# A recommendation network with row gathers: VectorE operations rewritten to have one SBUF input, and the last block in another order

## The chip, the cores and the metric

The kernel runs on one core of a Trainium2 chip. The metric is the time of one launch on the device, in microseconds (us), as the median of several runs. Profiles are separate executions, taken by the hardware profiler; their time is longer than that of a timed run, and both are given below.

Engines are named as in the profile: PE is TensorE (PEld is its weight load), DVE is VectorE, ACT is ScalarE, POOL is GpSimd, SP is SyncE. SBUF is the memory on the core that all engines read, PSUM the one that TensorE writes its results to.

## What is computed

For each of 16,384 samples there are 69 user items and one label item. Each item is a row of 96 numbers of a table of 100,001 rows. A small network ("attention") gives each of the 69 rows a weight; the weighted rows are summed in ten groups, and a second network (the "top network") makes one number of the ten sums and the label's row. Cut from the reference:

```python
FG = [20, 20, 10, 10, 2, 2, 2, 1, 1, 1]          # fields in each of the ten groups, 69 in all

def _dice(x, alpha, eps):
    p = jax.nn.sigmoid(_bn_eval(x, eps))          # _bn_eval: x / sqrt(1 + eps)
    return (alpha * (1.0 - p) + p) * x

u = emb[batch_user]                               # 16384 x 69 x 96
ql = emb[batch_label[:, 0]]
q = jnp.broadcast_to(ql[:, None, :], u.shape)
z = jnp.concatenate([q, u, q - u, q * u], axis=-1)
h = _dice(z @ W1 + b1, a1, EPS_DICE)              # 64 wide
att = (h @ W2 + b2) @ W3 + b3                     # one weight for each row
eff = (batch_user < ITEM_NUM)[..., None]          # the table's last row counts as zero
pre = jnp.where(eff, u * att, 0.0)
pooled = jnp.einsum('gf,bfe->bge', window, pre).reshape(u.shape[0], G * E)
x = jnp.concatenate([pooled, ql], axis=-1)        # 1056 wide
h = _dice(_bn_eval(x @ Wf1 + bf1, EPS_BN), af1, EPS_DICE)     # 200
h = _dice(_bn_eval(h @ Wf2 + bf2, EPS_BN), af2, EPS_DICE)     # 80
return h @ Wf3 + bf3
```

## The kernel before

The samples are worked through in 32 blocks of 512. A block has 69 chunks of 512 rows: 64 "main" chunks of 8 samples with their first 64 fields each, and 5 "tail" (single-field) chunks, each with one of the last 5 fields of all 512 samples. Two chunks make a pair; there are 1104 pairs. Every chunk takes four gathers of 128 rows, each an indirect DMA that GpSimd issues: 8,832 for the users' rows and 128 for the labels'.

The program is written as one loop over steps. In step i the pairs are at different stages, and the order of the calls is the order on each engine:

```python
POOL_LAG = 8

def gather(dst, index):
    nc.gpsimd.indirect_dma_start(out=dst, out_offset=None, in_=emb,
        in_offset=bass.IndirectOffsetOnAxis(ap=index, axis=0))

def map_ids(n, ids):          # ids >= ITEM_NUM are moved on by one, to an appended row of zeros
    rows = ipool.tile([P, NT], I32, tag="rows", name=f"rows{n}")
    nc.vector.scalar_tensor_tensor(rows, ids[:, 0:NT], float(ITEM_NUM), ids[:, 0:NT], ALU.is_ge, ALU.add)
    return rows

def fetch(i):                 # upool has 14 buffers, so gathers can run ahead of TensorE
    ...
    for j in range(2):
        n, k = chunk(2 * i + j)
        for t in range(4):
            gather(u[:, 4 * j + t, :], rows[n][:, 4 * k + t : 4 * k + t + 1])
            nc.tensor.transpose(ptr[:, t * P : (t + 1) * P], u[:, 4 * j + t, :], ident)     # L308
        ...                   # L311/L318: quT = ptr * q (DVE); L319: uT = ptr (ACT)

def hidden(i, ph, uT, quT):   # attention's first layer and its dice
    ...                       # L326: four matmuls into ph
    nc.scalar.activation(y, ph, AF.Sigmoid, scale=S_DICE)                 # L328
    nc.scalar.activation(y, y, AF.Identity, bias=a1c, scale=na1c)         # L329
    nc.vector.tensor_mul(y, ph, y)                                        # L330

def attend_tail(i, j, y, uT): # weights of a tail chunk, and its weighted rows
    nc.tensor.matmul(pa, vrep[...], y[...], start=True, stop=True)        # L346
    nc.vector.scalar_tensor_tensor(pres[n][:, k - NMAIN, :], pa, bb[0:E], uT[:, j, :], ALU.add, ALU.mult)  # L347

def spread(b, row):           # weights of four pairs, beside each row of the groups' matrix R
    ...                       # L353: four transposes into pt (PSUM)
    nc.vector.tensor_scalar(w, pt[:, :, :, 0:2].rearrange("p t k j -> p k j t"), bb, None, ALU.add)   # L356
    nc.vector.tensor_tensor(                                              # L359, both inputs in SBUF
        rw.rearrange("p k j t g -> p (k j t) g"),
        R.rearrange("p (k g) -> p k g", k=1).to_broadcast([P, 32, 2 * G]),
        w.rearrange("p k j (t o) -> p (k j t) o", o=1).to_broadcast([P, 32, 2 * G]), ALU.mult)
    return rw

def pool(i, u, rw):           # weighted sums of the main chunks of a pair; the PSUM pool has one buffer
    ...                       # L376: matmuls of u with rw into pa; L385/L391: pooled <- pa (DVE)

def top1(n, h, part, p1):     # half h of the 200 outputs, in four parts of four matmuls
    ...                       # L406: matmuls over pooled, the label's row and pres, 512 columns
    nc.vector.tensor_scalar(x1, p1, S_BN, sbf1[h], ALU.mult, ALU.add)     # L410
    nc.scalar.activation(g1, x1, AF.Sigmoid, scale=S_DICE)                # L411
    nc.scalar.activation(g1, g1, AF.Identity, bias=af1c[h], scale=naf1c[h])   # L412
    nc.vector.tensor_mul(x1, x1, g1)                                      # L413, both inputs in SBUF
# top2: L420 matmuls, L421 to L424 as L410 to L413; top3: L429 matmul, L431 bias, L432 output
```

The loop, with cuts. `seed` fills the accumulator of a pair with its label's share; `attend_rows` (L337, L339) makes the rows that `spread` turns:

```python
for n in range(NBLK):
    first, end = n * NCH // 2, ((n + 1) * NCH - 1) // 2
    if n > 0:
        at(first - 24, ...load_ids...); at(first - 21, ...map_ids...); at(first - 14, ...head_gather...)
        ...
    for s, work in enumerate(top_steps(n)):       # 8 parts of top1, then top2, then top3
        at(end + POOL_LAG + 4 + s, work)
for i in range(NPAIR + POOL_LAG + 16):
    if 0 <= i - 1 < NPAIR: phs[i - 1] = seed(i - 1)
    if 0 <= i - POOL_LAG < NPAIR: pool(i - POOL_LAG, ...)
    ...        # attend_rows for pair i - 3 (each fourth step), attend_tail for i - 3, spread for i - 4 (each fourth)
    if 0 <= i - 2 < NPAIR: ys[i - 2] = hidden(i - 2, ...)
    if i < NPAIR: u, uT, quT = fetch(i)
    for work in plan.pop(i, []): work()
```

A last point of the setup: the five single-field chunks' weights V are worked out once, in 45 VectorE operations with two SBUF inputs (L222) in the first 12 steps.

Of the kernel before, what the change touches and what calls it, by code (L numbers as in the profile page):

```python
# [59 lines left out]
POOL_LAG = 8  # L60


@with_exitstack
def rec_kernel(
    ctx: ExitStack,
    tc: tile.TileContext,
    idx: bass.AP,
    emb: bass.AP,
    W1: bass.AP,
    b1: bass.AP,  # L70
# [33 lines left out]

    def map_ids(n, ids):

        rows = ipool.tile([P, NT], I32, tag="rows", name=f"rows{n}")
        nc.vector.scalar_tensor_tensor(rows, ids[:, 0:NT], float(ITEM_NUM), ids[:, 0:NT], ALU.is_ge, ALU.add)
        return rows

    ids, rows = {0: load_ids(0)}, {}
    rows[0] = map_ids(0, ids[0])

# [72 lines left out]
    bf3c = column(bf3, "bf3c", 1)  # L186
    naf1c = [one_minus(t, f"naf1c{i}") for i, t in enumerate(af1c)]
    naf2c = one_minus(af2c, "naf2c")
    sbf1 = []
    for i in range(2):  # L190
        t = const.tile([DH, 1], F32, name=f"sbf1_{i}")
        nc.vector.tensor_scalar_mul(t, bf1c[i], S_BN)
        sbf1.append(t)
    sbf2 = const.tile([D2, 1], F32, name="sbf2")
    nc.vector.tensor_scalar_mul(sbf2, bf2c, S_BN)

# [28 lines left out]

    def gather(dst, index):
        nc.gpsimd.indirect_dma_start(  # L227
            out=dst,
            out_offset=None,
            in_=emb,  # L230
            in_offset=bass.IndirectOffsetOnAxis(ap=index, axis=0),
        )

    def chunk(c):

        return divmod(c, NCH)

    def head_gather(n):

        q = bpool.tile([P, NQ, E], F32, tag="q", name=f"q{n}")  # L240
        for k in range(NQ):
            gather(q[:, k, :], ids[n][:, NT + k : NT + k + 1])
        return q
# [31 lines left out]
    def seed(i):  # L275

        ph = ps_h.tile([P, 512], F32, tag="h", name=f"ph{i}")
        nc.tensor.matmul(ph, zrow[:, 0:P], zrow, start=True, stop=False)  # L278
        (n0, k0), (n1, k1) = chunk(2 * i), chunk(2 * i + 1)
        if n0 == n1 and k1 < NMAIN:  # L280
            nc.scalar.copy(  # L281
                ph.rearrange("h (s f) -> h s f", f=FM), by_field(cs[n0][0][:, k0 * NS : (k0 + 1) * NS])
            )
        elif n0 == n1 and k0 >= NMAIN:
            nc.scalar.copy(ph, cs[n0][1])
        else:
            for j, (n, k) in enumerate([(n0, k0), (n1, k1)]):
                lo, hi = j * H1, (j + 1) * H1
                if k < NMAIN:
                    nc.scalar.copy(  # L290
                        ph[lo:hi].rearrange("h (s f) -> h s f", f=FM),
                        by_field(cs[n][1][lo:hi, k * NS : (k + 1) * NS]),
                    )
                else:
                    nc.scalar.copy(ph[lo:hi], cs[n][1][lo:hi, :])
        return ph

    def fetch(i):
# [4 lines left out]
        for j in range(2):  # L303
            n, k = chunk(2 * i + j)
            ptr = ps_tr.tile([E, 512], F32, tag="tr", name=f"ptr{i}_{j}")
            for t in range(4):
                gather(u[:, 4 * j + t, :], rows[n][:, 4 * k + t : 4 * k + t + 1])
                nc.tensor.transpose(ptr[:, t * P : (t + 1) * P], u[:, 4 * j + t, :], ident)  # L308
            q = qTs[n % 2][0:E]
            if k < NMAIN:  # L310
                nc.vector.tensor_tensor(  # L311
                    quT[:, j, :].rearrange("e (s f) -> e s f", f=FM),
                    ptr.rearrange("e (s f) -> e s f", f=FM),
                    by_field(q[:, k * NS : (k + 1) * NS]),
                    ALU.mult,
                )
            else:
                nc.vector.tensor_tensor(quT[:, j, :], ptr, q[:, 0:BLK], ALU.mult)  # L318
            nc.scalar.copy(uT[:, j, :], ptr)  # L319
# [29 lines left out]
    def spread(b, row):  # L349

        pt = ps_x.tile([P, 4, 4, 32], F32, tag="x", name=f"patt{b}")
        for t in range(4):
            nc.tensor.transpose(pt[:, t].rearrange("p k j -> p (k j)"), row[:, t * P : (t + 1) * P], ident)  # L353
        rw = rpool.tile([P, 4, 2, 4, 2 * G], F32, tag="rw", name=f"rw{b}")
        w = rpool.tile([P, 4, 2, 4], F32, tag="w", name=f"w{b}")
        nc.vector.tensor_scalar(  # L356
            w, pt[:, :, :, 0:2].rearrange("p t k j -> p k j t"), bb, None, ALU.add
        )
        nc.vector.tensor_tensor(  # L359
            rw.rearrange("p k j t g -> p (k j t) g"),  # L360
            R.rearrange("p (k g) -> p k g", k=1).to_broadcast([P, 32, 2 * G]),
            w.rearrange("p k j (t o) -> p (k j t) o", o=1).to_broadcast([P, 32, 2 * G]),
            ALU.mult,
        )
        return rw

    def pool(i, u, rw):
# [6 lines left out]
        for j, n, k in todo:  # L374
            for t in range(4):
                nc.tensor.matmul(  # L376
                    pa[:, j, 2 * t : 2 * t + 2, :].rearrange("e n g -> e (n g)"),
                    u[:, 4 * j + t, :],
                    rw[:, i % 4, j, t, :],
                    start=True,  # L380
# [8 lines left out]
        else:  # L389
# [3 lines left out]
            )  # L393

    KTOP = G + 1 + NTAIL

    def top1(n, h, part, p1):

        if part == 0:
            p1 = ps_m.tile([DH, BLK], F32, tag="m", name=f"p1_{n}_{h}")  # L400
        for k in range(part * KTOP // 4, (part + 1) * KTOP // 4):
            if k <= G:
                w, x = wf1[:, k], pooled[n][:, k, :] if k < G else qTs[n % 2][0:E, 0:BLK]
            else:
                w, x = V[:, k - G - 1], pres[n][:, k - G - 1, :]
            nc.tensor.matmul(p1, w[:, h * DH : (h + 1) * DH], x, start=(k == 0), stop=(k == KTOP - 1))  # L406
        if part < 3:
            return p1
        x1, g1 = x1s[n][:, h, :], xpool.tile([DH, BLK], F32, tag="g1", name=f"g1_{n}_{h}")
        nc.vector.tensor_scalar(x1, p1, S_BN, sbf1[h], ALU.mult, ALU.add)  # L410
        nc.scalar.activation(g1, x1, AF.Sigmoid, scale=S_DICE)  # L411
        nc.scalar.activation(g1, g1, AF.Identity, bias=af1c[h], scale=naf1c[h])  # L412
        nc.vector.tensor_mul(x1, x1, g1)  # L413

    def top2(n):
        x2 = xpool.tile([D2, BLK], F32, tag="x2", name=f"x2_{n}")
        g2 = xpool.tile([DH, BLK], F32, tag="g1", name=f"g2_{n}")[0:D2]
        p2 = ps_m.tile([D2, BLK], F32, tag="m", name=f"p2_{n}")
        for i in range(2):
            nc.tensor.matmul(p2, wf2[:, i, :], x1s[n][:, i, :], start=(i == 0), stop=(i == 1))  # L420
        nc.vector.tensor_scalar(x2, p2, S_BN, sbf2, ALU.mult, ALU.add)  # L421
        nc.scalar.activation(g2, x2, AF.Sigmoid, scale=S_DICE)
        nc.scalar.activation(g2, g2, AF.Identity, bias=af2c, scale=naf2c)
        nc.vector.tensor_mul(x2, x2, g2)  # L424
        return x2

    def top3(n, x2):
        p3 = ps_m.tile([1, BLK], F32, tag="m", name=f"p3_{n}")
        nc.tensor.matmul(p3, wf3, x2, start=True, stop=True)  # L429
        res = xpool.tile([1, BLK], F32, tag="res", name=f"res{n}")  # L430
        nc.vector.tensor_scalar(res, p3, bf3c, None, ALU.add)  # L431
        nc.sync.dma_start(out=out_v[n : n + 1], in_=res)  # L432

# [3 lines left out]

    def top_steps(n):


        def half(h, part):
            if h == 0 and part == 0:
                x1s[n] = xpool.tile([DH, 2, BLK], F32, tag="x1", name=f"x1_{n}")
            p1s[n] = top1(n, h, part, p1s.get(n))

        steps = [lambda h=h, part=part: half(h, part) for h in range(2) for part in range(4)]
        steps.append(lambda: x2s.__setitem__(n, top2(n)))
        steps.append(lambda: top3(n, x2s.pop(n)))
        return steps
# [7 lines left out]
    for n in range(NBLK):  # L457
        first, end = n * NCH // 2, ((n + 1) * NCH - 1) // 2
        if n > 0:
            at(first - 24, lambda n=n: ids.__setitem__(n, load_ids(n)))  # L460
            at(first - 21, lambda n=n: rows.__setitem__(n, map_ids(n, ids[n])))
            at(first - 14, lambda n=n: qs.__setitem__(n, head_gather(n)))
            at(first - 11, lambda n=n: head_turn(n, qs.pop(n)))
            at(first - 9, lambda n=n: cs.__setitem__(n, head_row(n)))
        for s, work in enumerate(top_steps(n)):
            at(end + POOL_LAG + 4 + s, work)
    for f in range(NTAIL):
        at(2 + 2 * f, lambda f=f: tail_weights(f))

    with tc.manual_schedule():  # L470
# [3 lines left out]
        for i in range(NPAIR + POOL_LAG + 16):  # L474
            if 0 <= i - 1 < NPAIR:
                phs[i - 1] = seed(i - 1)
            if 0 <= i - POOL_LAG < NPAIR:
                k = i - POOL_LAG
                pool(k, us.pop(k), rws[k // 4])
                if k % 4 == 3:  # L480
                    rws.pop(k // 4)
            if 0 <= i - 3 < NPAIR and (i - 3) % 4 == 3:
# [13 lines left out]
            if 0 <= i - 2 < NPAIR:  # L496
                ys[i - 2] = hidden(i - 2, phs.pop(i - 2), *hs[i - 2])
            if i < NPAIR:
                for j in range(2):
# [56 lines left out]
```

## Time and profile before

| what | value |
|---|---|
| timed runs, median of 3 | 11350.36 us (11344.71 to 11351.59) |
| profiled execution, span | 13499.4 us |
| first and last gather start in the profile | 3.3 and 13368.4 us |
| mean granted clock of TensorE in the profile | 0.658 of full speed |
| HBM read in the profile | 446 MB, 33 GB/s |

How to read it: the profiler's page gives the span and each engine's busy time first, then the span in 40 slices, then the chain of work that ended last. A group is one line of the kernel on one engine: out<-in by the program's names, how many, then busy time and mean duration of one after the bar, and after the second bar the engine's idle time just before them with what ended it. "issue" is idle time that nothing in the profile ended. The two matrix instructions of one fp32 matmul are counted apart.

### The profile page before, as it was taken

The numbers are of one execution on the slowest core, as the hardware profiler recorded it, in microseconds if no ns is written. First come the engines' busy times: TensorE is split into PE (matmuls) and PEld (weight loads), VectorE is DVE, ScalarE is ACT, GpSimd is POOL, SyncE is SP. The second block draws the span as 40 slices with busy tenths as digits, with TensorE's granted clock in tenths as the row PEclk, the third lists the DMA queues.
The fourth block names the chain that finished last, engine by engine and source line by source line (L and its number), as shares of the span: only waits on it lengthen the run. The fifth ranks groups of instructions, "written<-read, shape, count | busy, mean of one in ns | idle before, by whom it ended". The sixth has DMA issues, their size and how long they took to land.

```text
span 13499.4 us, 108113 instructions
## 1 busy us (share of the span) xinstructions
PE 10109.4 (75%) x41348; PEld 5068.4 (38%) x41348; DVE 3172.4 (24%) x5424; ACT 3740.6 (28%) x6086; POOL 8525.6 (63%) x8966
## 2 busy tenths in 40 slices
PE   4777777778777776777777777777778777787778
PEld 2333333334333333333333333333333333343334
DVE  2222222222222222222222222222222222222222
ACT  1222222223222222222222222222222222232222
POOL 6666666666666666666666666666666666666664
PEclk5666666666666677666666666766666666666657
DMA  1111111111111111111111111111111111111111
GB/s 37 34 34 35 33 34 33 34 35 34 34 34 34 34 34 33 33 34 34 33 34 34 34 34 35 34 33 33 33 35 34 34 33 34 35 34 33 34 32 22
DMA packets 295008, 453.59 MB, mean 34 GB/s; under 512 B 145952, under 2 KB 151104, under 8 KB 294496
## 3 DMA queue, kind: packets, MB, share of 16 engines
q0 software_dynamic: 286720, 440.98, 15.5%
q8 instruction: 331, 5.42, 0.2%
q1 hardware_dynamic: 6142, 4.77, 0.1%
q14 instruction: 181, 1.48, 0.0%
q10 hardware_dynamic: 1634, 0.94, 0.0%
HBM read 446.04 MB, written 0.07 MB: 33 GB/s over the span
## 4 chain that ended last, share of the span: by engine, by line
PE 62%; another core or an unknown queue 15%; issue 12%; ACT 5%; DVE 5%; POOL 1%; DMA 0%; DVEq 0%; POOLq 0%; ACTq 0%
PE ph L326 22%; PE acc L376 15%; PE ptr L308 9%; PE p L406 5%; PE prow L337 4%; PE ph L278 4%; DVE y L330 3%; ACT y L329 2%; PE patt L353 2%; ACT y L328 1%; PE pa L346 1%; DVE quT L311 1%; ACT uT L319 1%; POOL u L227 1%
## 5 line engine op out<-in xcount | busy, mean ns | idle before, releaser
L227 POOL DMA_INDIRECT u<-in_emb,rows x8832 | 8401.6, 951 | 4802.4 <-issue 2351.7
L376 PEld LDWEIGHTS acc<-rw,u 128*96 128x96 f32 x16384 | 2185.5, 230 | 2828.8 <-issue 2828.2
L278 PE MATMUL ph<-zrow 1*128 1x512 bf16 x1104 | 532.2, 482 | 2654.8 <-DVE y L330 1760.5
L319 ACT COPY uT<-ptr 96x512 f32<-96x512 f32 x2208 | 1285.2, 582 | 3713.4 <-DVE quT L311 2616.7
L376 PE MATMUL acc<-rw,u 128*96 128x20 f32 x16384 | 2298.9, 292 | 1.8 <-DVE rw L359 1.3
L308 PEld LDWEIGHTS ptr<-ident,u 128*96 128x96 f32 x8832 | 1312.6, 167 | 1912.8 <-issue 1547.8
L308 PE MATMUL ptr<-ident,u 128*96 128x128 f32 x8832 | 1785.7, 362 | 326.1 <-issue 247.9
L326 PE MATMUL ph<-uT,A 96*64 96x512 f32 x4416 | 1954.0, 955 | 27.4 <-issue 26.7
L326 PE MATMUL ph<-quT,w 96*64 96x512 f32 x4416 | 1915.7, 909 | 54.5 <-issue 53.2
L328 ACT ACTIVATE y<-ph 128x512 f32<-128x512 f32 x1104 | 659.4, 597 | 4602.9 <-remote 2107.1
L330 DVE TENSOR_TENSOR y<-ph,y 128x512 f32<-128x512 f32 x1104 | 763.7, 692 | 4689.6 <-ACT y L329 2396.5
L311 DVE TENSOR_TENSOR quT<-ptr,qT 96x512 f32<-96x512 f32 x2048 | 1340.0, 680 | 1866.9 <-remote 887.1
L385 DVE COPY pooled<-acc 96x160 f32<-96x160 f32 x1008 | 430.6, 427 | 2811.6 <-remote 1020.7
L326 PEld LDWEIGHTS ph<-quT,w 96*64 96x64 f32 x4416 | 491.4, 202 | 1279.1 <-issue 1277.6
L329 ACT ACTIVATE y<-y,a1c,na1c 128x512 f32<-128x512 f32 x1104 | 897.4, 813 | 37.2
L281 ACT COPY ph<-cT 128x512 f32<-128x512 f32 x1008 | 591.4, 587 | 281.5 <-remote 75.0
L406 PE MATMUL p<-pooled,wf 96*100 96x512 f32 x1280 | 620.0, 625 | 6.3 <-issue 4.8
L337 PE MATMUL prow<-y,v 128*32 128x512 f32 x2208 | 546.6, 932 | 79.7 <-issue 41.3
L326 PEld LDWEIGHTS ph<-uT,A 96*64 96x64 f32 x4416 | 307.0, 183 | 766.4 <-issue 696.0
L339 ACT COPY row<-prow 128x512 f32<-128x512 f32 x276 | 161.4, 585 | 864.0 <-remote 345.4
L353 PE MATMUL patt<-ident,row 128*128 128x128 f32 x1104 | 267.9, 386 | 113.4 <-DVE pre L347 88.1
L406 PEld LDWEIGHTS p<-pooled,wf 96*100 96x100 f32 x1280 | 219.7, 181 | 270.1 <-issue 267.3
(71 smaller groups left out, 2535.6 us busy)
## 6 DMA issues: line engine op xcount, KB each, us to landing
u<-in_emb,rows POOLq DMA_INDIRECT x8832
ids<-in_idx SPq DMA_DIRECT2D x32, 140.0 KB
q<-in_emb,ids POOLq DMA_INDIRECT x128
wf<-in_Wf ACTq DMA_DIRECT2D x1, 825.0 KB
out<-res SPq DMA_DIRECT2D x32, 2.0 KB
w<-in_W SPq DMA_DIRECT2D x1, 96.0 KB
wf<-in_Wf ACTq DMA_DIRECT2D x1, 62.5 KB
a1c<-in_a SPq DMA_DIRECT2D x2, 0.2 KB
```

What stands on the lines that cost most here:

```text
L227: nc.gpsimd.indirect_dma_start(out=dst, out_offset=None, in_=emb, in_offset=bass.IndirectOffsetOnAxis(ap=index, axis=0),)
L278: nc.tensor.matmul(ph, zrow[:, 0:P], zrow, start=True, stop=False)
L308: nc.tensor.transpose(ptr[:, t * P : (t + 1) * P], u[:, 4 * j + t, :], ident)
L311: nc.vector.tensor_tensor(quT[:, j, :].rearrange("e (s f) -> e s f", f=FM), ptr.rearrange("e (s f) -> e s f", f=FM), by_field(q[:, k * NS ...
L319: nc.scalar.copy(uT[:, j, :], ptr)
L326: nc.tensor.matmul(ph[j * H1 : (j + 1) * H1, :], w, x[:, j, :], start=False, stop=last)
L328: nc.scalar.activation(y, ph, AF.Sigmoid, scale=S_DICE)
L329: nc.scalar.activation(y, y, AF.Identity, bias=a1c, scale=na1c)
L330: nc.vector.tensor_mul(y, ph, y)
L337: nc.tensor.matmul(pr[32 * k : 32 * (k + 1), :], v2, y, start=True, stop=True)
L376: nc.tensor.matmul(pa[:, j, 2 * t : 2 * t + 2, :].rearrange("e n g -> e (n g)"), u[:, 4 * j + t, :], rw[:, i % 4, j, t, :], start=True, st ...
L406: nc.tensor.matmul(p1, w[:, h * DH : (h + 1) * DH], x, start=(k == 0), stop=(k == KTOP - 1))
```

## The change

It has two purposes. First, no VectorE operation in the blocks is to have two inputs in SBUF. The index mapping L108 goes, as a second table `rows` on the device has a row of zeros in the place of the last one (the labels still use `emb`). `spread` works straight from PSUM, and the dice of the top network takes its value from PSUM twice, with scale and bias in the sigmoid and in the weights. Second, the last block gets another order, to shorten what is left after the last gather: its five tail chunks come after 48 main chunks and not at its end; its top network runs in two halves of 256 samples, the first of them from step NPAIR - 7; and the poolings of four pairs (1096 to 1099) are called in step 1103, ahead of the last `fetch`.

```diff
+EARLY = 3 * NMAIN // 4
-    def map_ids(n, ids):
-        ...
-    ids, rows = {0: load_ids(0)}, {}
-    rows[0] = map_ids(0, ids[0])
+    ids = {0: load_ids(0)}
...
+    def dice_weights(b, a, name):
+        sb, sa, sna = (const.tile(list(b.shape), F32, name=f"{name}_{k}") for k in range(3))
+        nc.vector.tensor_scalar_mul(sb, b, S_BN * S_DICE)
+        nc.vector.tensor_scalar_mul(sa, a, S_BN)
+        nc.vector.tensor_scalar(sna, a, -S_BN, S_BN, ALU.mult, ALU.add)
+        return sb, sa, sna
...
     def chunk(c):
-        return divmod(c, NCH)
+        n, k = divmod(c, NCH)
+        if n == NBLK - 1 and k >= EARLY:
+            k = NMAIN + k - EARLY if k < EARLY + NTAIL else k - NTAIL
+        return n, k
...
-                gather(u[:, 4 * j + t, :], rows[n][:, 4 * k + t : 4 * k + t + 1])
+                gather(rows, u[:, 4 * j + t, :], ids[n][:, 4 * k + t : 4 * k + t + 1])
...
-        rw = rpool.tile([P, 4, 2, 4, 2 * G], F32, tag="rw", name=f"rw{b}")
-        w = rpool.tile([P, 4, 2, 4], F32, tag="w", name=f"w{b}")
-        nc.vector.tensor_scalar(w, pt[...], bb, None, ALU.add)
-        nc.vector.tensor_tensor(rw..., R..., w..., ALU.mult)
+        rw = rpool.tile([P, 16, 2, 2 * G], F32, tag="rw", name=f"rw{b}")
+        for j in range(2):
+            nc.vector.scalar_tensor_tensor(
+                rw[:, :, j, :],
+                pt.rearrange("p t k j -> p (t k) j")[:, :, j : j + 1].to_broadcast([P, 16, 2 * G]),
+                bb,
+                R.rearrange("p (o g) -> p o g", o=1).to_broadcast([P, 16, 2 * G]),
+                ALU.add,
+                ALU.mult,
+            )
...
+    def dice(x, g, p, b, weights):
+        sb, sa, sna = weights
+        nc.scalar.activation(g, p, AF.Sigmoid, bias=sb, scale=S_BN * S_DICE)
+        nc.scalar.activation(g, g, AF.Identity, bias=sa, scale=sna)
+        nc.vector.scalar_tensor_tensor(x, p, b, g, ALU.add, ALU.mult)
...
-    def top1(n, h, part, p1):
+    def top1(n, cols, h, part, p1):          # top2 and top3 get cols as well
...
-        nc.vector.tensor_scalar(x1, p1, S_BN, sbf1[h], ALU.mult, ALU.add)
-        nc.scalar.activation(g1, x1, AF.Sigmoid, scale=S_DICE)
-        nc.scalar.activation(g1, g1, AF.Identity, bias=af1c[h], scale=naf1c[h])
-        nc.vector.tensor_mul(x1, x1, g1)
+        dice(x1s[n][:, h, cols], g1, p1, bf1c[h], dice1[h])
...
-        for s, work in enumerate(top_steps(n)):
-            at(end + POOL_LAG + 4 + s, work)
+        if n < NBLK - 1:
+            for s, work in enumerate(top_steps(n, slice(0, BLK))):
+                at(end + POOL_LAG + 4 + s, work)
+        else:
+            for s, work in enumerate(top_steps(n, slice(0, BLK // 2))):
+                at(NPAIR - 7 + s, work)
+            for s, work in enumerate(top_steps(n, slice(BLK // 2, BLK))):
+                at(end + POOL_LAG + 1 + s, work)
...
-            if 0 <= i - POOL_LAG < NPAIR:
+            if 0 <= i - POOL_LAG < NPAIR and i - POOL_LAG in us:
...
+            if i == NPAIR - 1:
+                for k in range(i - 7, i - 3):
+                    pool(k, us.pop(k), rws[k // 4])
             if i < NPAIR:                        # fetch(i)
...
-        "emb": np.concatenate([x["emb"], np.zeros((1, E), np.float32)], axis=0),
+        "emb": x["emb"],
+        "rows": np.concatenate([x["emb"][:ITEM_NUM], np.zeros((1, E), np.float32)], axis=0),
```

## The prediction

> **What bounds the kernel now.** I began with the page: busy time, the row of granted clock, the shares of the chain, and the group of the gathers.
>
> ```profile
> span 13499.4 us, 108113 instructions
> ...
> PE 10109.4 (75%) x41348; PEld 5068.4 (38%) x41348; DVE 3172.4 (24%) x5424; ACT 3740.6 (28%) x6086; POOL 8525.6 (63%) x8966
> ...
> PEclk5666666666666677666666666766666666666657
> ...
> PE 62%; another core or an unknown queue 15%; issue 12%; ACT 5%; DVE 5%; POOL 1%; DMA 0%; DVEq 0%; POOLq 0%; ACTq 0%
> ...
> L227 POOL DMA_INDIRECT u<-in_emb,rows x8832 | 8401.6, 951 | 4802.4 <-issue 2351.7
> ```
>
> Read alone, this says TensorE. But the profiled execution took 13499 us and the timed ones 11350, so some bound of the profile is not that of the timed runs. The second view is that of the gathers' line: what one takes, and what ended GpSimd's idle time before it.
>
> ```profile
> L227 POOL DMA_INDIRECT u<-in_emb,rows x8832: 939/947/1556, 8.6 to 13368.4; - x197
> ...
>   issue: 2390.5, 7830
>   PE acc L376: 860.1, 160
>   remote: 755.3, 239
>   PE ptr L308: 447.0, 177
> ```
>
> The reader is to see that one gather is busy 0.947 us (the median) and that the usual idle time before the next, which nothing else ends ("issue"), is 2390.5/7830 = 0.305 us: a pace of 1.252 us. Counted from start to start over the whole trace, 8,093 of the 8,959 intervals lie under 1.262 us and their mean is 1.2507 us. At that pace the 8,959 intervals (8,832 user rows and 128 labels, less one) last 11205 us. The waits for TensorE to free a buffer (acc, ptr) are what the profiled execution has on top. My reading: **the timed runs are bound by GpSimd's pace of issuing gathers**, and TensorE binds only under the profiler. 11205 + 3.3 us before the first gather + 1.8 us (13501.2 profiled time less 13499.4 span) = 11210. Of 11350 there remain **140 us** that any change of this kind can reach.
>
> **What those 140 us are.** Part one shows in the timeline, where a gather is held:
>
> ```profile
> 267.04 0.95 POOL L227 DMA_INDIRECT u<-in_emb,rows  x1 [0.31 <-issue]
> 267.67 0.25 DVE L356 TENSOR_SCALAR w<-patt,bb 128x32 f32<-128x32 f32 x1 [1.72 <-remote]
> ...
> 267.95 0.83 DVE L359 TENSOR_TENSOR rw<-R,w 128x640 f32<-128x640 f32 x1
> 268.29 1.31 POOL L227 DMA_INDIRECT q<-in_emb,ids  x1 [0.30 <-issue]
> 269.90 0.95 POOL L227 DMA_INDIRECT q<-in_emb,ids  x1 [0.30 <-issue]
> ```
>
> L359 was running when the gather began; the gather took 1.31 us instead of 0.95, and the next started 1.61 us after it. Of all gathers 174 took over 0.96 us, and 168 of those lie beside a VectorE operation with two inputs in SBUF. The groups of VectorE by shape give those operations, and L347 as a counterexample:
>
> ```profile
> L359 DVE TENSOR_TENSOR rw<-R,w 128x640 f32<-128x640 f32 x276 | 228.4, 828 | 9.5
> L347 DVE SCALAR_TENSOR_TENSOR pre<-pa,bb,uT 96x512 f32<-96x512 f32 x160 | 114.2, 736 | 136.3 <-PE pa L346 63.6 <-issue 31.1 <-remote 17.3
> ...
> L413 DVE TENSOR_TENSOR x<-x,g 100x512 f32<-100x512 f32 x64 | 44.5, 695 | 98.8 <-ACT g L412 63.3 <-ACT g L411 27.8 <-issue 7.7
> ...
> L424 DVE TENSOR_TENSOR x<-x,g 80x512 f32<-80x512 f32 x32 | 22.0, 688 | 49.4 <-ACT g L423 26.3 <-ACT g L422 13.9 <-issue 9.3
> ...
> L108 DVE SCALAR_TENSOR_TENSOR rows<-ids 128x276 int32<-128x276 int32 x32 | 13.8, 432 | 0.6 <-DMA ids<-in_idx 0.6
> ```
>
> Beside L347 (one input in PSUM, one in SBUF, a column as scalar) 158 gathers lie, and none is longer. The excess of intervals beside two-SBUF operations sums to **51 us**: 40 for L359, 9 for L413 and L424, 2 for L108, under 1 for the weights V at the start (L222). In the profile some 9% of the gathers stood waiting anyway, where a hold costs nothing; scaled by 8,960/8,166 (all gathers over the intervals under 1.4 us) it is 56 us.
>
> Part two is the tail. The chain of waits ends thus:
>
> ```profile
> 13456.28 15.89 PE p L406 x32
> 13472.19 0.76 DVE x L410
> 13473.00 13.99 PE p L406 x32
> 13487.02 0.76 DVE x L410
> ```
>
> The last gather starts at 13368.43 and the span ends at 13499.4, but TensorE is then five pairs of chunks late under the profiler. Its last transposes (L308) begin at 13419.6; from there to the end it is 79.8 us. The least distance from a gather's start to its transpose in the trace is 2.4 us. Without backlog the tail is therefore about **82 us**. 56 + 82 = 138 of 140: the account closes within 2 us, which is the best support for the reading.
>
> [...] the trace has 0.50 for the stretch 13419.6 to 13456.2 and 0.86 for what follows. [...]
>
> **The change part by part.** *Two-SBUF operations.* L359's one operation becomes two of 320 elements with one input in PSUM. From L347, 736 ns for 512 at 0.96 elements per ns leaves 203 ns fixed, so 203 + 333 = 536 ns each, 1.07 us for both against 239 + 828 before: VectorE is no busier. L108 goes, as the table itself now ends in a row of zeros. In the top network the scale and bias move into the sigmoid, and the product takes its first input from PSUM: 96 operations of about 745 ns go (L410, L421), and none of the remaining ones has two SBUF inputs. Only V's 45 at the start stay, about 1 us. **56 becomes 1: 55 us less.**
>
> *The tail, at the trace's durations.* From the start of the last transposes the new order needs: transposes 1.9; seed and wait 1.0; two hidden layers 2 x 3.65; one piece of the first half's top network 1.7; sigmoid, line and product 2.3; rows 1.9, their copy 0.6, their transposes 0.95, two weightings 1.1, hand-overs 0.4; four poolings of 2.7 with a copy between (the accumulator has one buffer) 0.5 each, 12.8. Then the second half of samples: 64 matrix instructions of 256 columns, half of 0.43, 13.8; a wait of 1.75 for the first activation, as PSUM is held until the product; activation 1.75, second layer 0.65, its activation 1.75, third 0.95, bias 0.5, output 2.2. Sum 55.3 against 79.8: **24.5 us less**. (256 columns: ScalarE 0.63 and 0.81 become 0.42 and 0.60, VectorE 0.75 becomes 0.48, each less 256 elements at the engine's rate.)
>
> *What comes back.* The last chunks now are ones that need pooling, and the four moved poolings with a piece of the top network stand ahead of the last transposes: 12.8 + 1.7 on a step of about 10.1 at half clock, 24.6 us, while the step's eight gathers last 10.0. The last transposes may be 14.6 us late; at full clock (6.4 + 1.9 + 8.2 = 16.5) 6.5 us. I take 12. **Net 12 to 13 us less; a tail of about 69.**
>
> Sum: 11210 + 1 + 69 + 2 unexplained = 11282. A hold costs up to 0.6 us, by where in a gather's cycle the operation starts; in timed runs that place may be steadier and dearer, so I shade it to **11280 us**.
>
> **Rivals.** (1) *TensorE bounds the timed runs too.* For it: 75% busy, 62% of the chain. Then the holds are hidden and only some tail is saved: 11320 to 11350. Against it: gathers and tail add up without it. (2) *The new order overloads TensorE in the last block.* At half clock each of the steps with a piece of the first half's top network costs 10 + 3.4 against 10.0 of gathers; six steps put it 20 us behind, the tail's gain is gone or turned: 11290 to 11310. For it: the half clock in the tail. (3) *The holds are dearer when timed*, as no backlog of TensorE scatters L359's place in the cycle: up to 90 us of the 140, then 11240. (4) The longer hold of PSUM by the top network makes TensorE wait each block; the next piece stands one step, some 10 us, later, so I give it nothing.
>
> **Range and chances.** Rival 3 sets 11240; rival 1 with a part of 2 sets 11325. Faster by over 2% would need under 11123, below the 11205 of the gathers alone: 0.01. Slower by over 2% needs 227 us of new waiting that no row hints at: 0.02. Within 2%: 0.97.
>
> **What would show it right or wrong.** Gathers over 0.96 us gone but for the first 250 us; the pace still 1.25; the new weighting operations near 0.54 us each; fewer than 60 us from the last transposes to the end. The profile's own span says little, as TensorE binds there. Wrong if single-PSUM operations hold gathers too, if the pace itself moves, or if the time falls under 11210, which would break the account.

## The result, and the profile after

The changed kernel takes **11267.35 us** (median of 6 runs, 11262.03 to 11275.01), the kernel before 11350.98 us beside it (6 runs, 11344.71 to 11353.67): a ratio of **0.9927, 95% interval 0.9914 to 0.994**, or 84 us less. The prediction was 11280, with a range of 11240 to 11325.

First, the page of the kernel after: span, busy times, granted clock and shares of the chain.

```profile
span 11265.5 us, 109062 instructions
...
PE 9779.7 (87%) x41418; PEld 4767.8 (42%) x41418; DVE 3092.5 (27%) x5303; ACT 3770.0 (33%) x6092; POOL 8463.8 (75%) x8966
...
POOL 37%; PE 32%; issue 17%; DMA 11%; ACT 1%; DVE 1%; POOLq 0%
```

This time the profiled execution is as long as the timed ones; that a profile takes longer, as said at the start, held for the first one only. "another core or an unknown queue", 15% of the chain before, is gone. TensorE is now busy for 87% of a shorter span, and still GpSimd has the largest share of the chain: a busy share is no bound. Next, the gathers' line, to be held against the same view of before (longest gather 1556 ns, 860.1 us of waits for acc):

```profile
L225 POOL DMA_INDIRECT u<-in_rows,ids x8832: 940/945/1078, 8.5 to 11195.0; - x197
...
  issue: 2479.1, 8137
  DMA u<-in_rows,ids: 117.6, 386
```

No gather of a user's rows is longer than 1.078 us, and after the first 127 us, in which V is made, no gather of any kind is longer than 0.962 us. The usual idle time before one is 2479.1/8137 = 0.305 us, and those waits that the trace puts down to TensorE last 0.3 us too, at the longest. The groups of VectorE by shape that answer to L359 and L413:

```profile
L357 DVE SCALAR_TENSOR_TENSOR rw<-patt,bb,R 128x320 f32<-128x320 f32 x552 | 277.7, 544 | 80.2 <-PE patt L354 74.2
...
L400 DVE SCALAR_TENSOR_TENSOR x<-p,bf1c,g 100x512 f32<-100x512 f32 x62 | 46.5, 750 | 242.9 <-ACT g L399 242.9
```

Beside L357 lie 435 gathers and beside L400 107; only one of them takes over 0.962 us, and it falls in the first 127 us.

And the chain of waits at the end (start, duration, engine, what), where the line of before had pieces of 15.89 and 13.99 us:

```profile
11208.38 1.75 PE ptr L309 x8
...
11236.14 10.58 PE p L413 x32
11246.74 0.48 ACT g L398
...
11248.42 8.85 PE p L413 x32
...
11262.83 0.47 DVE res L432
```

The eight last transposes stand at 11208.38. Only half of the samples' top network is left behind the poolings, in two pieces of 10.58 and 8.85 us (x32 are 16 fp32 matmuls, two matrix instructions each).

### The profile page after: what moved, and what is told of

The parts are those of the page before. It is cut to its first block, busy times and chain, and to the rows that moved or that the text cites. A ratio compares the mean times of both kernels' runs of the same rounds, so it can differ in the third digit from the quotient of the medians.

```text
span 11265.5 us, 109062 instructions
## 1 busy us (share of the span) xinstructions
PE 9779.7 (87%) x41418; PEld 4767.8 (42%) x41418; DVE 3092.5 (27%) x5303; ACT 3770.0 (33%) x6092; POOL 8463.8 (75%) x8966
## 4 chain that ended last, share of the span: by engine, by line
POOL 37%; PE 32%; issue 17%; DMA 11%; ACT 1%; DVE 1%; POOLq 0%
POOL u L225 36%; DMA u<-in_rows,ids 11%; PE ph L327 11%; PE acc L376 8%; PE p L413 3%; PE ptr L309 3%; PE prow L338 2%; PE ph L279 2%; POOL q L225 1%; PE pa L347 1%; ACT y L330 1%; PE patt L354 1%; DVE y L331 1%; ACT y L329 1%; PE pc L268 0%
## 5 line engine op out<-in xcount | busy, mean ns | idle before, releaser
L225 POOL DMA_INDIRECT u<-in_rows,ids x8832 | 8342.1, 945 | 2690.8 <-issue 2440.4
L309 PE MATMUL ptr<-ident,u 128*96 128x128 f32 x8832 | 2068.5, 357 | 1279.7 <-DMA u<-in_rows,ids 1256.1
L309 PEld LDWEIGHTS ptr<-ident,u 128*96 128x96 f32 x8832 | 1234.0, 156 | 3208.2 <-DMA u<-in_rows,ids 1641.4
L376 PEld LDWEIGHTS acc<-rw,u 128*96 128x96 f32 x16384 | 2064.6, 219 | 505.7 <-issue 501.0
L376 PE MATMUL acc<-rw,u 128*96 128x20 f32 x16384 | 2176.7, 283 | 3.7 <-DVE pooled L385 3.1
L331 DVE TENSOR_TENSOR y<-ph,y 128x512 f32<-128x512 f32 x1104 | 763.4, 692 | 4502.0 <-ACT y L330 4398.1
L329 ACT ACTIVATE y<-ph 128x512 f32<-128x512 f32 x1104 | 659.6, 598 | 3836.1 <-PE ph L327 3835.7
L327 PE MATMUL ph<-uT,A 96*64 96x512 f32 x4416 | 1801.1, 908 | 0.0
L327 PE MATMUL ph<-quT,w 96*64 96x512 f32 x4416 | 1686.1, 854 | 0.0
L330 ACT ACTIVATE y<-y,a1c,na1c 128x512 f32<-128x512 f32 x1104 | 897.1, 813 | 37.2
L279 PE MATMUL ph<-zrow 1*128 1x512 bf16 x1104 | 527.6, 478 | 165.3 <-DVE y L331 163.1
L413 PE MATMUL p<-pooled,wf 96*100 96x512 f32 (+1 forms) x1320 | 651.7, 638 | 2.2 <-DVE x L400 1.7
L338 PE MATMUL prow<-y,v 128*32 128x512 f32 x2208 | 452.2, 903 | 0.3 <-DVE y L331 0.3
L413 PEld LDWEIGHTS p<-pooled,wf 96*100 96x100 f32 x1320 | 238.3, 189 | 272.6 <-issue 263.9
L413 PE MATMUL p<-pre,V 96*100 96x512 f32 (+1 forms) x660 | 310.9, 604 | 0.0
## 6 DMA issues: line engine op xcount, KB each, us to landing
wf<-in_Wf ACTq DMA_DIRECT2D x1, 62.5 KB
```

What stands on the lines that cost most here:

```text
L225: nc.gpsimd.indirect_dma_start(out=dst, out_offset=None, in_=table, in_offset=bass.IndirectOffsetOnAxis(ap=index, axis=0),)
L327: nc.tensor.matmul(ph[j * H1 : (j + 1) * H1, :], w, x[:, j, :], start=False, stop=last)
L338: nc.tensor.matmul(pr[32 * k : 32 * (k + 1), :], v2, y, start=True, stop=True)
L376: nc.tensor.matmul(pa[:, j, 2 * t : 2 * t + 2, :].rearrange("e n g -> e (n g)"), u[:, 4 * j + t, :], rw[:, 4 * t + i % 4, j, :], start=Tru ...
```

## Experiments

In four groups; kernels of one group ran on one chip, and ratios are to the kernel before beside them. The kernel before took 11341 us beside the first group and 11359 beside the fourth, but 13601 and 13536 us beside the second and third, where TensorE was the bound (before gathers, 1017 us of waits for acc in `dose_two`, 1104 in `dose_one` and 1053 in `after_again`, as against 860 in the first profile of before, 2.4 in `again` and 1.5 in the kernel after), so that holds of gathers could be read there from traces only, not from times.

**The account.** For each trace I add up the starts of the 8,960 gathers. Pace is the mean of the intervals under 1.262 us. Held is what the longer intervals have above that pace. Tail is the last gather's start to the end. 3.3 us + 8,959 x pace + held + tail is the span by the way the terms are made, so that the sum comes out is no evidence; what a change does to each term is. The changed kernel less `again`: held 71.7 us less, tail 11.1 less, pace 6.3 more (0.7 ns x 8,959): 76.5 less, and the spans differ by 76.1.

| kernel | span us | pace ns | longer intervals, held us | tail us | start of the last transpose after the last gather's start us | from there to the end us |
|---|---|---|---|---|---|---|
| before (`again`) | 11341.6 | 1248.3 | 237, 73.6 | 81.5 | 2.4 | 79.1 |
| `spread` | 11293.3 | 1248.3 | 99, 25.9 | 80.8 | 3.2 | 77.6 |
| `ports` | 11273.7 | 1248.3 | 24, 1.9 | 85.2 | 2.5 | 82.7 |
| `order` | 11339.6 | 1249.8 | 251, 76.0 | 63.4 | 9.1 | 54.4 |
| after | 11265.5 | 1249.0 | 28, 1.9 | 70.4 | 14.7 | 55.7 |
| `earlier_again` | 11268.9 | 1250.2 | 36, 2.4 | 62.5 | 9.9 | 52.6 |

### First group: the kernel before again, and the change taken apart

**`again`**: the kernel before, unchanged.

> The kernel before, unchanged, in a new profile. The first profile took 13499 us where the timed runs took 11351. If the profiler slows TensorE as such (my reading in the prediction), this one is again near 13500. If that profile was one bad execution, its span is near 11350, the pace of the gathers is 1.25 us, and the gathers held beside operations with two SBUF inputs add up to what the account needs: 11351 less the gathers (11197) less a tail of about 82 leaves about 72 us.

11343.32 us, with a profile. The profiler does not make TensorE the bound: this is the same kernel under the same profiler, 2158 us shorter than the first profile. Its page and the gathers' line:

```profile
span 11341.6 us, 108113 instructions
```

```profile
L227 POOL DMA_INDIRECT u<-in_emb,rows x8832: 940/944/1597, 8.5 to 11260.1; - x197
```

Of its gathers 231 took over 0.96 us, 225 of them beside a VectorE operation with two SBUF inputs. What L359 does depends on where in the gather's cycle it starts. Three cases from the timeline of this run:

```profile
5316.78 0.83 DVE L359 TENSOR_TENSOR rw<-R,w 128x640 f32<-128x640 f32 x1
5316.83 1.60 POOL L227 DMA_INDIRECT u<-in_emb,rows  x1 [0.30 <-issue]
...
5388.67 0.94 POOL L227 DMA_INDIRECT u<-in_emb,rows  x1 [0.30 <-issue]
5388.73 0.83 DVE L359 TENSOR_TENSOR rw<-R,w 128x640 f32<-128x640 f32 x1
...
9588.54 0.90 DVE L359 TENSOR_TENSOR rw<-R,w 128x640 f32<-128x640 f32 x1
9588.58 0.94 POOL L227 DMA_INDIRECT u<-in_emb,rows  x1 [0.30 <-issue]
```

Started 0.05 us ahead of the gather, L359 holds it for 0.66 us; started 0.06 us behind it, not at all, and L359 isn't held either. Between the two L359 waits: in the third case it starts 0.04 us ahead, takes 0.90 us instead of 0.83, and the gather isn't held. For L359, by its start after the last gather's start: up to 0.5 us, a mean hold of 1 ns at most; from 0.7 to 0.8 us 200 ns; from 0.9 to 1.0 us 280; from 1.1 to 1.2 us 586.

**`ports`**: the first part of the change alone. Edit on the kernel after:

```diff
-EARLY = 3 * NMAIN // 4
+EARLY = NCH                    # chunks in the order of before
-        if n < NBLK - 1: ... else: ...   # top network of the last block in halves
+        for s, work in enumerate(top_steps(n, slice(0, BLK))):
+            at(end + POOL_LAG + 4 + s, work)
-            if i == NPAIR - 1: ...       # the four moved poolings
```

> Only the first part of the change: no operation with two SBUF inputs, the old order of the last block. Theory of the holds: 55 to 72 us less than before, 11279 to 11296, and no gather over 0.96 us after the first 250 us. Rival (the gain comes from the end): at most 15 us less, about 11340.

11270.18 us, ratio 0.9935 (0.9922 to 0.9949): 71 us less than before by the medians, 74 by the ratio. Of 73.6 us held, 1.9 are left; after the first 127 us no gather is longer than 0.962 us.

**`order`**: the second part alone: the kernel after with L108, the `spread` and the dice of before, and the new order kept.

```diff
-            nc.vector.scalar_tensor_tensor(rw[:, :, j, :], pt..., bb, R..., ALU.add, ALU.mult)   # twice
+        nc.vector.tensor_scalar(w, pt..., bb, None, ALU.add)
+        nc.vector.tensor_tensor(rw..., R..., w..., ALU.mult)
-        nc.vector.scalar_tensor_tensor(x, p, b, g, ALU.add, ALU.mult)
+        nc.vector.tensor_mul(x, x, g)    # with x = S_BN * p + b ahead of the sigmoid
```

> Only the second part: the last block in the new order, operations with two SBUF inputs kept. Theory of the holds: 12 us less than before, about 11339, with the holds as before. Rival (the gain comes from the end): 70 to 84 us less, 11267 to 11281.

11330.72 us, 0.9991 (0.9985 to 0.9998): 10 us less. The held 76.0 us are all there. The profiled execution, 11341.38 us, is one of the slowest of the 21: its tail is 18.1 us shorter than in `again`, and its longer pace took 13.4 us (1.5 ns x 8,959) of that. By the ratios the parts gain 74 and 10 us and the whole change 83: they add up, though the intervals of the first part and of the whole are 15 us wide on each side.

**`spread`**: on the kernel before, only L356 and L359 replaced by the two operations from PSUM.

```diff
-        nc.vector.tensor_scalar(w, pt..., bb, None, ALU.add)
-        nc.vector.tensor_tensor(rw..., R..., w..., ALU.mult)
+        for j in range(2):
+            nc.vector.scalar_tensor_tensor(rw[:, :, j, :], pt..., bb, R..., ALU.add, ALU.mult)
```

> The kernel before with the weighting alone (L359) made from PSUM; the index mapping and the top network keep their two SBUF inputs, the last block its order. By the profile's shares 40 of 51 us of holds: 43 to 56 us less, 11295 to 11308. If the three kinds of operation matter by their number alone (276 of 404), about the same; if the dice of the top network matters more than its share, under 30 us less.

11290.45 us, 0.9952 (0.9938 to 0.9965): 51 us less by the medians, 54 by the ratio. In `again`, with each lengthened interval put down to one operation, L359 had 50.9 us of hold beside it and L413 18.1. Here the longest gather is 1451 ns, and what is left, 25.9 us, lies mostly beside the top network's product, 20.2 us for this group (of `spread`):

```profile
L412 DVE TENSOR_TENSOR x<-x,g 100x512 f32<-100x512 f32 x64 | 44.3, 692 | 98.8 <-ACT g L411 98.8
```

So over 60% of the whole gain is one line. `ports`, which also makes the dice from PSUM and has no index mapping, is 20 us faster than `spread`.

### Second group: a dose of one kind of operation

**`dose_two`**: the kernel after with 276 useless products, both inputs in SBUF, behind each weighting.

```diff
+        nc.vector.tensor_tensor(spare..., R..., ident[:, 0 : 2 * G]..., ALU.mult)      # 560 elements
```

> The changed kernel plus one useless VectorE operation after each weighting, 276 in all, of 560 elements with both inputs in SBUF [...]. Theory of the holds: it holds gathers as L359 did; at an even spread over the cycle 0.16 us each, 45 us, and up to 0.5 us each, 140 us, if its place in the cycle is bad: 20 to 140 us more than the changed kernel. Rival (VectorE's busy time or its chain counts, not the inputs): the same as the next kernel.

**`dose_one`**: the same with one input in PSUM.

```diff
+        nc.vector.scalar_tensor_tensor(spare[:, 0:512]..., pt..., bb, ident..., ALU.add, ALU.mult)
```

> The same, but the useless operation has one input in PSUM and one in SBUF and 512 elements, also some 740 ns. Theory of the holds: no gather is held, under 5 us more than the changed kernel. Rival: as much as the kernel before this one.

Their times are 13650.97 us, 1.0041 (1.0027 to 1.0055), and 13659.14, 1.0041 (1.0025 to 1.0056): equal, as gathers were not the bound, so the expected difference in time did not show. The traces tell the two apart. The operations last 729 and 740 ns. In `dose_two` 142 of the 348 gathers beside L367 are over 0.96 us, with 49 us of hold; in `dose_one` none of 358. One case of each from the timelines, first `dose_two`, then `dose_one`:

```profile
661.13 0.73 DVE L367 TENSOR_TENSOR spare<-R,ident 128x560 f32<-128x560 f32 x1
...
661.44 1.24 POOL L227 DMA_INDIRECT u<-in_rows,ids  x1 [0.30 <-issue]
...
662.98 0.94 POOL L227 DMA_INDIRECT u<-in_rows,ids  x1 [0.30 <-issue]
```

```profile
323.61 0.74 DVE L367 SCALAR_TENSOR_TENSOR spare<-patt,bb,ident 128x512 f32<-128x512 f32 x1
324.02 0.94 POOL L227 DMA_INDIRECT u<-in_rows,ids  x1 [0.30 <-issue]
...
325.26 0.94 POOL L227 DMA_INDIRECT u<-in_rows,ids  x1 [0.30 <-issue]
```

Both gathers begin while L367 runs. Beside two SBUF inputs the gather takes 0.30 us more; beside one, nothing. The holds follow the second SBUF input and not VectorE's being busy.

**`dice`**: on the kernel before, only the dice of the top network from PSUM.

```diff
-        nc.vector.tensor_scalar(x1, p1, S_BN, sbf1[h], ALU.mult, ALU.add)
-        ...
-        nc.vector.tensor_mul(x1, x1, g1)
+        dice(x1, g1, p1, bf1c[h], dice1[h])      # top2 alike
```

> The kernel before with the top network's dice alone from PSUM (96 operations with two SBUF inputs less, and 96 VectorE operations less in all). From the second profile of the kernel before, where its gathers were held 18 us beside L413 and 2 us beside L424: 20 us less than before, up to 4 us given back at the end, where PSUM is held longer. By the first profile, 9 us less.

13654.57 us, 1.0022 (1.0007 to 1.0036). No gain; with TensorE as the bound this says nothing of its holds. `spread`'s trace has their size.

### Third group: parts of the new order

**`after_again`**: the kernel after, unchanged.

> The changed kernel, unchanged, so that the next ones have it beside them on the same chip: 0.9927 of before, some 83 us less.

13567.61 us, 1.0019 (1.0003 to 1.0034): **where TensorE binds, the change gains nothing.** The waits of this run (engine, tile, line <- what ended it: us in total, times, longest):

```profile
PEld acc L376 <- issue: 2815.1, 1032, 16.6
...
ACT y L329 <- remote: 2094.4, 240, 26.1
...
POOL u L225 <- PE acc L376: 1053.2, 187, 40.6
```

Gathers wait up to 40.6 us at a time for TensorE to free buffers. TensorE itself stands idle for up to 24.9 us (L279, until y L331). Idle times of over 5 us stand 205 times in its records in the first profile of before, never in those of the kernel after above; the mean granted clock here is 0.667 against 0.707 there. The operations of VectorE and ScalarE last as long in both (L329 0.60 us, L330 0.81, L331 0.69). What opens these gaps stays open: the row names "remote", a wait whose end the profile doesn't tell, and this trace has 10,615 updates of TensorE's semaphore for 13,219 instructions that make one (13,215 in that of the kernel after).

**`nomove`**: the kernel after without the four moved poolings; **`whole`**: with the last block's top network in one piece of 512 samples from step end + POOL_LAG + 1; **`earlier`**: tail chunks after 36 main chunks, first half from step NPAIR - 10.

```diff
 nomove
-            if i == NPAIR - 1: ...               # the four moved poolings
 whole
+            at(end + POOL_LAG + (4 if n < NBLK - 1 else 1) + s, work)     # slice(0, BLK) for all blocks
 earlier
+EARLY = NMAIN // 2 + 4
+                at(NPAIR - 10 + s, work)         # the first half of samples
```

> The changed kernel without the four moved poolings: they go back to steps 1104 to 1107, behind the last transposes. By my reading of the trace TensorE reaches the last transposes some 13 us late because of them, so this moves 13 us from before the last transposes to after them: within 4 us of the changed kernel, with the last transposes about 3 us after the last gather. If TensorE stood idle there, as the change assumes: up to 10 us more.

> The changed kernel with the last block's top network whole, behind the last poolings: 14 us of matrix work and some 4 us of longer activations are added behind the last transposes, less the pieces that now delay them (about 5 us): 12 to 16 us more than the changed kernel. If the new order gains by the chunks' order instead, under 4 us more.

> The changed kernel with the single-field chunks after 36 main chunks in place of 48, and the first half of the top network three steps earlier, so that it ends in step 1103. Three pieces of 1.9 to 3.4 us leave the last two steps: 4 to 9 us less than the changed kernel. If TensorE is as late anyway (half clock), no difference.

13572.91 us, 1.0029 (1.0016 to 1.0042); 13603.18, 1.0045 (1.0028 to 1.0063); 13577.63, 1.0032 (1.002 to 1.0044). Beside `after_again` only `whole` stands out, though the two intervals overlap. Counted as in the table, its last transpose is 71.8 us from the end against 56.2 in `after_again`: 15.6 us for what the halves keep from the end, of which 5.1 come back, as that transpose stands 66.5 us after the last gather and not 71.6. In `nomove` it stands 58.3 us after the last gather, 13.3 sooner, as expected; but the rest takes 58.4 us, only 2.2 longer and not 13. The granted clock was higher there (1.00 against 0.78 in the 20 us ahead of the last transposes), so what the moved poolings are worth stays open; nothing here shows a gain from them.

### Fourth group

**`earlier_again`**: the kernel `earlier` once more, where gathers bind.

> The same kernel as in the run named earlier (single-field chunks after 36 main chunks, first half of the top network three steps sooner), once more, as in that run TensorE was far behind the gathers everywhere and the end could not show. Where the kernel before takes about 11345 us: the last transposes 4 to 9 us less late than the changed kernel's 13.2 us, and 0.9919 to 0.9924 of before against 0.9927. Where it takes about 13550 us: no difference from the changed kernel, about 1.002 to 1.003.

11275.57 us, 0.9927 (0.9913 to 0.994): the ratio of the change itself. Its last transpose is 4.8 us less late than that of the changed kernel, as expected, and its tail 7.9 us shorter; its pace is 1.2 ns longer (10.8 us). Whether it is any better stays open; no version tried is shown to beat the changed kernel.

## Why the prediction was right, and where it was not

**"The timed runs are bound by GpSimd's pace of issuing gathers": right for the runs compared.** In the six traces of the table the gathers' waits beyond their pace are 1.9 to 76.0 us of some 11,300, and taking the holds away shortened the time by what they had cost (71.7 us less held by the traces of `again` and `ports`, 71 us less time by the medians). In `again` a transpose follows its gather by 5.2 us (the median); in the first profile by 72.

**"TensorE binds only under the profiler": wrong.** `again` is a profile without it, and the third group has it in timed runs. I had seen that the two times disagreed and took the first explanation at hand.

**The holds: the operations right, the size not.** "51 us, scaled to 56" was 73.6 in `again`, and the change took 71.7 of them, not 55. The terms that were too small: L359, put at 40 us, had 50.9; L413 with L424, put at 9, had 20.1. The count of operations is the same; the place in the gather's cycle isn't: of the 276 L359, 117 start 0.8 us or more after the last gather's start in `again`, 100 in the first profile (a mean hold of 184 and 139 ns). So rival 3 has the holds dearer, at 74 us and not 90, but its reason, that a late TensorE scatters them, is not borne out: in `dice` a transpose follows its gather by 73 us, as in the first profile, and the weighting (L361 there) still holds gathers for 51 us. What sets the place stays open.

**The floor: 15 us too high.** "1.2507 x 8959" was the pace of that one execution. It is 1249.0 ns in the trace of the kernel after, which is (1.2507 - 1.2490) x 8,959 = 15 us less. So "the account closes within 2 us, which is the best support" was two errors that met: against `again` the gathers were put 21.5 us too high (2.4 ns x 8,959) and the holds 17.6 too low. `ports` and `spread` are the support that this was not. The predicted time after the change has the holds in it only as the 1 us that is left, so that it came out says nothing of their size; the predicted gain of 70 us was 84.

**The tail: right in its sum, not in its terms.** From the last transpose: 24.5 us less predicted, 79.1 - 55.7 = 23.4 measured. Tail: 69 and 70.4. But the matrix work of the second half, predicted as 13.8 us at 0.215 us an instruction, took 10.58 + 8.85 = 19.4 us: at the granted clocks of 0.67 and 0.81 in these two pieces some instructions took 0.427 us and others 0.216. And the stretch before it, predicted as 32.0 us with two hidden layers of 3.65 us each, took 27.8, though two pieces of the first half's top network stood in it and not one: the hidden layers took 1.87 and 1.92. The delay of the last transposes, 12 predicted and 14.7 - 2.4 = 12.3 measured, was a pick between two estimates, 6.5 at full clock and 14.6 at half (the first profile has a granted clock of 0.50 from 13419.6 to 13456.2 us and 0.86 from there to the end), so partly luck: in the 20 us ahead of them the clock was 0.51 here, and in `order`, with the same order of work, 0.76 and the delay 6.7. At half width the activations take 0.48 and 0.61 us (0.42 and 0.60 predicted), the product 0.49 (0.48). By the means of the trace after, 256 elements less save ScalarE 213 ns (L398 687 to 474, L399 813 to 600) and VectorE 266 (L400 750 to 484). The new weighting takes 544 ns (536 predicted, an estimate with 0.96 elements per ns; the first profile's L413 and L359, 695 ns for 512 and 828 for 640, give 128/133 = 0.96).

**The sum again**, from the predicted 11282: pace -15, holds left +1 (1.9 for 1), tail +1.4, the "2 unexplained" -2: 11267.

**Rivals.** (1) TensorE as the bound: not in the runs compared, but in the second and third group, and there its consequence (holds hidden, nothing gained) held. (2) Overload in the last block: 12.3 us of delay, the figure already in the sum, and not 20. (3) Dearer holds: yes, but not for the reason given. (4) The longer hold of PSUM: before the gathers of the kernel after one wait is for p, of 0.3 us; `ports`, which has it in each block, gains what the holds cost.

**Who holds whom: the two sides are unequal.** In `again` 137 L359 hold a gather that begins more than 0.15 us before their end, each for what is left of it less 0.127 us (0.117 to 0.132). A gather holds L359 too, but only for a moment about its own start: the 18 that start between 43 ns ahead of a gather's start and 19 ns behind it take 836 to 899 ns instead of 825, and all end 854 to 857 ns after that start; their gathers take the usual 940 to 947 ns. One that starts 35 ns behind, or later in the gather, takes 825. So the longest wait of an L359 for a gather of 0.944 us was 0.075 us.

## What to carry to other kernels

Before reading a bound from a profile, compare its span with the timed runs; where they differ, profile again rather than explain the difference. Where GpSimd's gathers set the pace, look for VectorE operations with two SBUF inputs: here an L359 of 0.83 us cost not its duration but what was left of it when the next gather began, less 0.127 us, and with one input straight from PSUM, and the index mapping gone, the holds fell from 73.6 to 1.9 us (`again`, `ports`). Sum a pace from the same trace as its holds, and don't take a sum that closes for a proof: undo the parts one at a time.

## What the runs showed that was not expected

The pace is constant within an execution (each twentieth of the gathers within 0.3 ns of its mean) and differs between executions from 1248.1 to 1250.7 ns, whatever the kernel: 2.6 ns x 8,959 = 23 us. The difference lies in the gather itself (943.4 to 945.8 ns in the mean); the time between two stays at 304.7 to 304.9 ns. This alone is larger than what the new order gains, and what sets it stays open. And one kernel has two lengths, 11.3 and 13.6 ms, with idle gaps of TensorE in the longer; the traces show the gaps and not their cause. The chip alone doesn't set the length: the second and the fourth group have the same chip number on record, and the kernel before took 13601 us beside one and 11359 beside the other.
